# A decoder layer on one core: the feed-forward's low products behind a switch of TensorE, and the third norm's last step on GpSimd

## The chip, the core and the metric

The kernel runs on one core of one Trainium2 chip. A core has five engines with instruction streams of their own: TensorE (PE in the profile; its weight loads are PEld), VectorE (DVE), ScalarE (ACT), GpSimd (POOL) and SyncE (SP), which only issues transfers here. They wait for one another by semaphores. Sixteen DMA engines move data between the chip's memory and the on-chip memory, and they also bring the engines' instructions: the profile lists that traffic as queues of the kind "instruction". The metric is the device time of one execution in microseconds, and the time of a kernel is the median of its runs.

## The reference, cut to what matters

The layer computes, for 4 batches of 1024 tokens with 512 features in float32, an attention with 32 heads, a gated convolution, and a feed-forward, each added to its input and followed by a layer norm without learned scale. The part around the change is the feed-forward and the third norm:

```python
scale = jnp.maximum(act_scale, 1e-05)
x_int = jnp.clip(jnp.round(x / scale), -QB, QB)          # QB = 127
x_dq = jnp.nan_to_num(x_int * scale, nan=0.0, posinf=10000.0, neginf=-10000.0)
w = ternary_weight.astype(jnp.float32) - 1.0
return jnp.einsum('bsi,oi->bso', x_dq, w) + bias
...
x = _layernorm(x + _L0_ffn_ref(x, ternary_weight, bias, act_scale), axis=-1)
```

`ternary_weight` is an int32 array; the inputs drawn for it are 0, 1 or 2, so `w` is -1, 0 or 1.

## The kernel before, in words

`attention` takes the first 1700 us. `tail` does the rest, and it is written as one program of steps whose order is set by hand: `tail` enters a manual schedule, so each engine runs its instructions in the order in which the Python code issues them. A counter `now` is raised by `step()`, and `after(n, work)` puts work off by n steps; work that is due is issued at the end of the step, behind what the step itself issued.

`tail` goes twice over two batches, (0, 2) and then (1, 3). Each pass first runs the gated convolution: 32 gates for the two batches, one a step. `gate` (L1195 to L1216) gives TensorE four groups of 16 products into two pairs of PSUM buffers (`pc` and `pa`, two of each), then VectorE four additions (L1209, L1212, L1213, L1215), then ScalarE a sigmoid or tanh (L1216). After four gates `combine` spreads GpSimd, VectorE and ScalarE work over the next steps. Between, GpSimd makes sums of the next convolution weights (`sum_taps`, L196).

In the first pass, `halves_of_w_f` is issued along with the gates, one part at each of steps 17, 19, 21 and 23 and its last at step 25. For a quarter f of the feed-forward's weights, GpSimd copies the weights into the rounded type float32r (`w_hi`, L255) and subtracts that from the weights (L256), so that the remainder stands in `w_f`; SP writes it out (L257) and reads it back as `w_lo` (L261), also float32r.

Then comes `feed_forward` for the pass's two batches: 16 tiles of 128 tokens. For tile k the order of issue is:

- `turn` of tile k+1: four transposes on TensorE of the quantised tile `xq` (L1288) and ScalarE's copy of them from PSUM as float32r (`xq_t`, L1290);
- `feed` of tile k: eight products into one PSUM buffer `pf` (two buffers, tag "o"), four with `w_hi` and four with `w_lo` (L1298);
- `quantise` of tile k+3: ScalarE rounds (L1281), and VectorE (the first three) or GpSimd clamps (L1282);
- roots and aggregates of a finished group (`third_norm`'s `first`: L1314, L138);
- `residual` of tile k: VectorE adds the input (L1303) and takes the moments (L1304).

`third_norm` normalises in groups of four tiles (smaller at the end of a pass). Its `finish(m)` writes the normalised tile in place and has SP send it out (L1337). For even m ScalarE computes it as an activation with the scale `rstd` and the bias `shift` (L1332); for odd m VectorE computes it (`normalised`, L142). The very last tile is fed, added and finished in two halves of 256 columns.

After the first feed-forward, TensorE goes on with `project_out` (L292), whose PSUM buffers are the same two of tag "o".

Of the kernel before, what the change touches and what calls it, by code (L numbers as in the profile page):

```python
# [8 lines left out]
F32 = mybir.dt.float32  # L9
F32R = mybir.dt.float32r  # L10
AF = mybir.ActivationFunctionType
ALU = mybir.AluOpType
# [50 lines left out]
class Handed:  # L63
# [76 lines left out]

    def normalised(self, dst, src, mv, rstd, t):
        self.nc.vector.tensor_scalar(  # L142
            dst, src, mv[:, t, 0:1], rstd[:, t : t + 1], ALU.subtract, ALU.mult
        )
# [101 lines left out]

    def halves_of_w_f(self, pool, dram):


        nc, w = self.nc, self.w_f  # L250
        self.w_hi = pool.tile([P, FT, D], F32R, tag="w_hi", name="w_hi")
        low_d = dram.tile([P, FT, D], F32, tag="w_low", name="w_low_d")

        def part(f):
            nc.gpsimd.tensor_copy(self.w_hi[:, f, :], w[:, f, :])  # L255
            nc.gpsimd.tensor_sub(w[:, f, :], w[:, f, :], self.w_hi[:, f, :].bitcast(F32))  # L256
            nc.sync.dma_start(low_d[:, f, :], w[:, f, :])  # L257

        def last():
            self.w_lo = self.shared.tile([P, FT, D], F32R, tag="w_f", name="w_lo")  # L260
            nc.sync.dma_start(self.w_lo.bitcast(F32), low_d)  # L261

        return [lambda f=f: part(f) for f in range(FT)] + [last]

# [874 lines left out]
def tail(ctx, tc, a, out, ident, eps, hand, dram):  # L1139
# [153 lines left out]
    def feed(b, t, cols=slice(0, D)):  # L1293
        pt = ps_o.tile([P, D], F32, tag="o", name=f"pf{b}_{t}_{cols.start}")[:, 0 : cols.stop - cols.start]
        for n, w in enumerate((hand.w_hi, hand.w_lo)):
            for f in range(FT):
                last = n == 1 and f == FT - 1
                nc.tensor.matmul(pt, xq_ts[b, t][:, f, :], w[:, f, cols], start=n == f == 0, stop=last)  # L1298
        return pt
# [6 lines left out]
    def third_norm(b, n0, n):  # L1306
# [19 lines left out]
        def finish(m):  # L1326
            t = order[m]
            n = 2 if (b, m) == (B - 1, NT - 1) else 1
            for h in range(n):
                part = y[:, t, h * D // n : (h + 1) * D // n]  # L1330
                if m % 2 == 0 or h == 1:
                    nc.scalar.activation(  # L1332
                        part, part, AF.Identity, bias=made[2][:, m : m + 1], scale=made[0][:, m : m + 1]
                    )
                else:
                    hand.normalised(part, part, mv3[b], made[0], m)
# [73 lines left out]
    for m, work in enumerate(scaling):  # L1410
        after(9 + m, work)
    for m, work in enumerate(hand.halves_of_w_f(bigs, dram)):
        after(17 + 2 * m, work)
# [81 lines left out]
```

## Time and profile before

| what | value |
|---|---|
| median of 3 runs | 2144.36 us (2143.28, 2144.36, 2148.23) |
| the profiled execution | 2147.72 us, span of the profile 2145.8 us |
| granted TensorE clock, mean | 0.998 |
| first feed-forward, first to last product | 1854.97 to 1895.0 us |
| second feed-forward, first to last product | 2099.99 to 2140.12 us |
| products with `w_hi` and with `w_lo` | 132 and 132 |

The page's first part gives each engine's busy time. The second cuts the span into 40 slices. The third lists the DMA queues with packets, megabytes and their share of the sixteen engines' span. The fourth follows the chain of work that ended last. The groups, in the fifth, collect instructions by line, engine and tile, with the mean time of one, and then the idle time of the engine ahead of them with what ended it. The timeline lists instructions in order of time; the bracket at a line's end is idle time ahead of it and what ended it. Windows give each engine's busy time in a stretch. Matmul ends are modelled, so that consecutive matmuls overlap in the listing: their start-to-start distance is what counts.

### The profile page before, as it was taken

To read this page: it belongs to the slowest core of one execution; us is meant where nothing else is said; L and a number is where in the kernel's file an instruction comes from. 1 tells how busy PE (TensorE), PEld (TensorE's weight loads), DVE (VectorE), ACT (ScalarE), POOL (GpSimd) and SP (SyncE) were. 2 spreads that over 40 slices of the span, in tenths; PEclk is the share of its full clock that TensorE was granted. 3 is DMA by queue.
4 is the path that set the end of the run, shared out by engine and by line. 5 is a ranking of instruction groups with operands and counts; after the bars stand their busy time and mean duration, and the time that the engine had idled before them with its cause. 6 is when DMAs were issued, how large, how long until landed. Compare 5 with 4: busy or idle time off the path is not lost.

```text
span 2145.8 us, 81983 instructions
## 1 busy us (share of the span) xinstructions
PE 2109.5 (98%) x35404; PEld 1528.9 (71%) x35404; DVE 1728.0 (81%) x3068; ACT 1388.3 (65%) x2771; POOL 977.5 (46%) x1298
## 2 busy tenths in 40 slices
PE   9999999999999999999999999999999999999998
PEld 6666666666666666666666666667766799858997
DVE  3678888888888888888888888888897566779667
ACT  1157777777777777777777777777777623521336
POOL 2562534333344334343533333645464369532773
PEclk9999999999999999999999999999999999999999
DMA  7513213332322233122313124422411243270222
GB/s 274 176 52 98 78 50 92 106 123 64 102 54 78 63 103 107 60 88 88 106 54 111 54 75 132 147 64 84 123 47 52 60 163 118 74 279 21 100 78 79
DMA packets 114538, 207.97 MB, mean 97 GB/s; under 512 B 36992, under 2 KB 37248, under 8 KB 114048
## 3 DMA queue, kind: packets, MB, share of 16 engines
q1 hardware_dynamic: 113456, 201.55, 29.4%
q8 instruction: 277, 4.54, 0.9%
q10 hardware_dynamic: 720, 1.18, 0.2%
q14 instruction: 85, 0.70, 0.1%
HBM read 132.41 MB, written 69.73 MB: 94 GB/s over the span
## 4 chain that ended last, share of the span: by engine, by line
PE 84%; DVE 13%; POOL 1%; issue 1%; ACT 1%; DMA 0%; SPq 0%; DVEq 0%; ACTq 0%; POOLq 0%
PE av L872 23%; PE nat L758 15%; PE st L835 10%; DVE mx L771 9%; PE part L60 9%; PE pa L1205 6%; PE pc L1205 6%; PE v L60 5%; PE po L60 3%; PE po L292 3%; PE fold L425 1%; PE proj L60 1%; PE pf L1298 1%; PE fold L60 1%; DVE stats L1304 1%
## 5 line engine op out<-in xcount | busy, mean ns | idle before, releaser
L771 DVE TENSOR_REDUCE mx<-nat 128x1 f32<-128x512 f32 x2048 | 1271.4, 684 | 197.8 <-PE nat L758 179.5
L844 ACT ACTIVATE at<-st 128x512 f32<-128x512 f32 x2016 | 1042.2, 603 | 320.5 <-PE st L835 316.6
L758 PE MATMUL nat<-qk 32*128 32x512 f32 x4096 | 712.1, 421 | 2.2 <-DVE v_sb L658 1.3
L835 PE MATMUL st<-qk 32*128 32x256 f32 x8064 | 681.7, 290 | 0.2
L835 PEld LDWEIGHTS st<-qk 32*128 32x128 f32 x8064 | 526.1, 184 | 4.9 <-issue 2.1
L835 PE MATMUL st<-qk,ones 2*128 2x256 f32 x4032 | 504.1, 287 | 0.0
L872 PE MATMUL av<-at,v_sb 128*32 128x256 f32 x8192 | 499.4, 382 | 4.2 <-ACT at L844 1.3
L758 PEld LDWEIGHTS nat<-qk 32*128 32x128 f32 x4096 | 328.6, 184 | 203.0 <-DVE mx L771 162.6
L872 PEld LDWEIGHTS av<-at,v_sb 128*32 128x32 f32 x8192 | 240.8, 109 | 182.3 <-DVE mx L771 25.2
L835 PEld LDWEIGHTS st<-qk,ones 2*128 2x128 f32 x4032 | 353.6, 183 | 0.0
L1216 ACT ACTIVATE u<-u,b_c 128x512 f32<-128x512 f32 x64 | 46.2, 723 | 159.6 <-DVE u L1215 155.7
L778 POOL CAST neg<-least 128x16 fp32r<-128x16 f32 x64 | 12.7, 199 | 216.0 <-DVE least L776 216.0
L885 DVE TENSOR_TENSOR o_sb<-av,o_sb 128x256 f32<-128x256 f32 x128 | 54.4, 425 | 61.6 <-PE av L872 61.2
L722 POOL TENSOR_TENSOR y<-y,extra 128x256 f32<-128x256 f32 (+8 forms) x152 | 73.5, 518 | 65.9 <-ACT extra L708 65.9
L1212 DVE SCALAR_TENSOR_TENSOR u<-pa,u 128x342 f32<-128x342 f32 x64 | 40.6, 634 | 67.5 <-PE pa L1205 66.3
L921 POOL TENSOR_TENSOR o_n<-o_sb,o_n 128x512 f32<-128x512 f32 x64 | 83.3, 1324 | 13.3 <-DVE u L1213 13.3
L450 POOL TENSOR_TENSOR extra<-extra,highs 128x512 f32<-128x512 f32 x62 | 79.6, 1284 | 5.0
L1205 PE MATMUL pa<-xf,w 128*128 128x171 f32 x512 | 80.4, 308 | 0.5 <-POOL w L196 0.5
L1205 PE MATMUL pc<-xf,w 128*128 128x171 f32 x512 | 79.8, 308 | 0.0
L883 ACT COPY o_sb<-av 128x256 f32<-128x256 f32 x128 | 48.1, 376 | 46.9 <-PE av L872 36.7
L1205 PEld LDWEIGHTS pa<-xf,w 128*128 128x128 f32 x512 | 76.0, 189 | 1.0 <-POOL w L196 1.0
L1205 PEld LDWEIGHTS pc<-xf,w 128*128 128x128 f32 x512 | 76.0, 189 | 0.0
(210 smaller groups left out, 2782.3 us busy)
## 6 DMA issues: line engine op xcount, KB each, us to landing
qk<-qk_d SPq DMA_DIRECT2D x96, 512.0 KB
qk_d<-highs SPq DMA_DIRECT2D x96, 256.0 KB
qk_d<-extra SPq DMA_DIRECT2D x96, 256.0 KB
u<-in_ctx SPq DMA_DIRECT2D x16, 1024.0 KB
xT<-in_xT SPq DMA_DIRECT2D x16, 512.0 KB
o_n<-rec_d SPq DMA_DIRECT2D x128, 64.0 KB
attn<-o_n SPq DMA_DIRECT2D x256, 32.0 KB
y<-in_x SPq DMA_DIRECT2D x16, 512.0 KB
```

Of the source, the lines that this page charges most:

```text
L60: nc.tensor.matmul(pt[r, :], lhsT(f)[:, r], rhs(f), start=f == 0, stop=f == tiles - 1)
L292: nc.tensor.matmul(pt, attn_t[:, f, t * P : (t + 1) * P], self.w_o[:, f, :], start=f == 0, stop=f == FT - 1)
L450: eng.tensor_sub(block, block, high)
L722: eng.tensor_add(c, c, x)
L758: lambda n=n, r=r, turn=turn: nc.tensor.matmul(pts[n], qk_sets[u % 3][turn][r : r + 32, qt * P : (qt + 1) * P], qk_sets[u % 3][2][r : r + ...
L771: nc.vector.tensor_reduce(mxs[u][:, qt, j, kh : kh + 1], pts[n], AX.X, ALU.max, negate=True)
L835: lambda st=st, k=k, n=n, left=left, right=right: nc.tensor.matmul(st[:, k * QW : k * QW + QW], left, right, start=n == 0, stop=n == 2),
L844: nc.scalar.activation(at, st, AF.Exp, scale=0.25)
L872: nc.tensor.matmul(av[32 * j : 32 * j + 32, :], v_sb[b % 2][:, kt, c * VW : c * VW + 32], ats[u, 2 * i + n // 2, j][:, n % 2 * QW : n % 2 ...
L885: nc.vector.tensor_add(o, av, o)
L921: nc.gpsimd.tensor_mul(part, o_sb[:, cols].rearrange("p (s e) -> p e s", e=2), part)
L1205: nc.tensor.matmul(pt, w[i][:, tap, o : o + P], xf[:, tap, i, :], start=i == 0, stop=i == FT - 1)
```

## The change

The change has three parts.

First, `halves_of_w_f` has VectorE take, for each quarter f of the remainders, the largest value and the negated smallest (two reductions of 128x512). A new step `compare`, at step 27, reduces these eight columns to one, multiplies that column on TensorE with the column `magic` of equal positive numbers, which sums it over the partitions into one number, and has VectorE compare it with nought into an int32 flag. A new step `read`, at step 29, loads the flag into a register of TensorE's instruction stream.

Second, `feed` issues a hint of a switch, then three products with `w_hi`, then a switch on the register with two arms. Arm 0 holds the fourth product with `w_hi` and nothing else. Arm 1 holds that product and the four with `w_lo`. Which arm runs is known only when the kernel runs; with the weights given, whole numbers from -1 to 1, the remainders are nought if the rounded type holds these numbers exactly. There are 33 calls of `feed`: 15 whole tiles and two halves in the second pass, 16 in the first.

Third, `finish` gives the last step of the third norm to GpSimd, as a subtraction and a multiplication with per-partition operands, for all tiles of batches 0, 1 and 2 and the first four of batch 3: 28 tiles, of which ScalarE and VectorE had 14 each. The last four tiles of batch 3 stay as they were.

```diff
-    def normalised(self, dst, src, mv, rstd, t):
-        self.nc.vector.tensor_scalar(
+    def normalised(self, dst, src, mv, rstd, t, eng=None):
+        (eng or self.nc.vector).tensor_scalar(
             dst, src, mv[:, t, 0:1], rstd[:, t : t + 1], ALU.subtract, ALU.mult
         )
...
-    def halves_of_w_f(self, pool, dram):
+    def halves_of_w_f(self, pool, dram, ps):
         nc, w = self.nc, self.w_f
+        lows = self.shared.tile([P, 2 * FT + 1], F32, tag="lows", name="lows")
+        flag = self.shared.tile([1, 1], mybir.dt.int32, tag="flag", name="flag")
...
             nc.gpsimd.tensor_copy(self.w_hi[:, f, :], w[:, f, :])
             nc.gpsimd.tensor_sub(w[:, f, :], w[:, f, :], self.w_hi[:, f, :].bitcast(F32))
             nc.sync.dma_start(low_d[:, f, :], w[:, f, :])
+            nc.vector.tensor_reduce(lows[:, f : f + 1], w[:, f, :], AX.X, ALU.max)
+            nc.vector.tensor_reduce(lows[:, FT + f : FT + f + 1], w[:, f, :], AX.X, ALU.min, negate=True)
+
+        def compare():
+            top = lows[:, 2 * FT : 2 * FT + 1]
+            nc.vector.tensor_reduce(top, lows[:, 0 : 2 * FT], AX.X, ALU.max)
+            pt = ps.tile([P, FT, P], F32, tag="t", name="any_low")[0:1, 0, 0:1]
+            nc.tensor.matmul(pt, top, self.magic, start=True, stop=True)
+            nc.vector.tensor_scalar(flag, pt, 0.0, None, ALU.is_gt)
+
+        def read():
+            engine = mybir.EngineType.PE
+            why = "a comparison gives nought or one"
+            self.any_low = {
+                engine: nc.values_load(
+                    flag, engines=[engine], min_val=0, max_val=1, skip_runtime_bounds_check_because=why
+                )
+            }
...
-        return [lambda f=f: part(f) for f in range(FT)] + [last]
+        return [lambda f=f: part(f) for f in range(FT)] + [last, compare, read]
...
         pt = ps_o.tile([P, D], F32, tag="o", name=f"pf{b}_{t}_{cols.start}")[:, 0 : cols.stop - cols.start]
-        for n, w in enumerate((hand.w_hi, hand.w_lo)):
-            for f in range(FT):
-                last = n == 1 and f == FT - 1
-                nc.tensor.matmul(pt, xq_ts[b, t][:, f, :], w[:, f, cols], start=n == f == 0, stop=last)
+        tc.switch_hint(hand.any_low, 2, label=f"low{b}_{t}_{cols.start}")
+        def product(w, f, start=False, stop=False):
+            nc.tensor.matmul(pt, xq_ts[b, t][:, f, :], w[:, f, cols], start=start, stop=stop)
+
+        for f in range(FT - 1):
+            product(hand.w_hi, f, start=f == 0)
+        for arm in tc.Switch(hand.any_low, n=2, hint=f"low{b}_{t}_{cols.start}"):
+            product(hand.w_hi, FT - 1, stop=arm == 0)
+            if arm:
+                for f in range(FT):
+                    product(hand.w_lo, f, stop=f == FT - 1)
         return pt
...
-                if m % 2 == 0 or h == 1:
+                if b != B - 1 or m < 4:
+                    hand.normalised(part, part, mv3[b], made[0], m, nc.gpsimd)
+                elif m % 2 == 0 or h == 1:
...
-    for m, work in enumerate(hand.halves_of_w_f(bigs, dram)):
+    for m, work in enumerate(hand.halves_of_w_f(bigs, dram, ps_t)):
         after(17 + 2 * m, work)
```

## The prediction

> **What bounds the kernel now.** I read the page first: busy times, DMA queues, the chain that ended last.
>
> ```profile
> PE 2109.5 (98%) x35404; PEld 1528.9 (71%) x35404; DVE 1728.0 (81%) x3068; ACT 1388.3 (65%) x2771; POOL 977.5 (46%) x1298
> q8 instruction: 277, 4.54, 0.9%
> PE 84%; DVE 13%; POOL 1%; issue 1%; ACT 1%; DMA 0%; SPq 0%; DVEq 0%; ACTq 0%; POOLq 0%
> ```
>
> TensorE (PE) carries the chain. Queue q8 is TensorE's code: 35404 products and as many weight loads over 277 packets are 256 instructions a packet, so a packet is one block of code (16 KB). 0.9% of sixteen engines over 2145.8 us is 309 us, or 1.1 us a packet. It is fetched while the code runs straight on, and nearly nothing waits for it (issue 1%).
>
> Next the two feed-forwards as windows (columns: TensorE, weight loads, DVE, ACT, POOL, clock, DMA share, GB/s), then the groups in the first and TensorE's timeline of one tile.
>
> ```profile
> 1854.97:1895.00 40.03, 37.31 (x187) 29.58 (x187) 35.36 (x79) 29.76 (x46) 18.16 (x20) 1.00 0.43 149
> 2099.99:2140.12 40.13, 37.42 (x194) 29.82 (x193) 35.66 (x79) 29.86 (x46) 18.09 (x19) 1.00 0.19 71
> ```
>
> ```profile
> L1303 DVE SCALAR_TENSOR_TENSOR y<-pf,sc,big 128x512 f32<-128x512 f32 x15 | 11.1, 739 | 1.5 <-PE pf L1298 1.5
> L1304 DVE BATCH_NORM_STATS2 stats<-y 128x6 f32<-128x512 f32 x15 | 10.4, 695 | 0.5
> L1282 POOL TENSOR_SCALAR xq<-xq 128x512 f32<-128x512 f32 x10 | 6.4, 641 | 8.5 <-ACT xq L1281 8.1
> L142 DVE TENSOR_SCALAR y<-y,mv,rstd 128x512 f32<-128x512 f32 x11 | 6.0, 561 | 0.1
> L1332 ACT ACTIVATE y<-y,shift,rstd 128x512 f32<-128x512 f32 x7 | 5.6, 806 | 0.7 <-DVE shift L1321 0.7
> ```
>
> ```profile
> 1870.82 0.60 PE L1288 MATMUL tr<-ident,xq 128*128 128x128 f32 x4
> 1871.18 1.16 PE L1298 MATMUL pf<-w_hi,xq_t 128*128 128x512 f32 x4
> 1872.18 1.09 PE L1298 MATMUL pf<-w_lo,xq_t 128*128 128x512 f32 x4
> 1873.11 0.60 PE L1288 MATMUL tr<-ident,xq 128*128 128x128 f32 x4
> ```
>
> A tile takes 2.29 us, start to start: transposes 0.36, high products 1.00, low ones 0.93. VectorE is close behind, 35.36 of 40.03 us busy.
>
> **The change, part by part.** *Removed:* the remainders of -1, 0 and 1 are nought if the rounding keeps whole numbers, as I assume; arm 0 runs. TensorE loses 128 products of 512 columns and 4 of 256: 31 tiles by 0.93 and two halves by 0.46, 29.8 us. That is a bound, not the gain: without them a tile needs 1.36 us of TensorE, while VectorE needs 0.74 + 0.69 and its share of aggregates, about 1.7.
>
> *Third norm's last step:* 28 tiles go to POOL, 14 from ACT (0.81 each), 14 from VectorE (0.53): 8 of each in the first feed-forward, 6 in the second. POOL's price lies between its clamp, 0.64, and its two-input addition in the same window, 1.34; I take 0.64, the same operation with two scalars. The first feed-forward gives POOL 18.16 + 16 x 0.64 = 28.4 us of 40 (39.6 by the high price); the clamp of a later tile queues behind it, and POOL now waits 8.1 us there for ACT. SP's output transfer waits for POOL instead. Hidden, gain on the path nought unless TensorE has become faster than VectorE.
>
> *The flag.* Eight reductions of 128x512 on VectorE (L771's 0.68 each, 5.5 us) in a stage where TensorE is the bound. Their place costs more: each pair stands in VectorE's order behind a gate's additions and waits for POOL's subtraction.
>
> ```profile
> 1803.01 0.88 DVE L1215 SCALAR_TENSOR_TENSOR u<-pa,u 128x513 f32<-128x513 f32 x1
> 1804.39 0.64 DVE L1209 TENSOR_TENSOR u<-pc,u 128x342 f32<-128x342 f32 x1 [0.49 <-PE pc L1205]
> 1807.38 1.28 POOL L256 TENSOR_TENSOR w_f<-w_f,w_hi 128x512 f32<-128x512 f32 x1
> 1819.73 1.98 PE L1205 MATMUL pa<-xf,w 128*128 128x171 f32 x10 [0.49 <-POOL w L196]
> ```
>
> The third pair would be due about 1804 and can't start before 1808.7; the gates' next additions queue behind it, ACT's gate functions behind those, POOL's `combine` behind these and its weight sums (L196) last, for which TensorE already waits 0.49 us. TensorE is two gates (9.3 us) ahead at most by its buffers. From 0 (all absorbed) to 8 us (two delays of 4 in full); I take 4, the middle, as the last row has no slack and the buffers have some. `compare`: TensorE's small product follows gate 27 at once but needs VectorE's 0.64 + 0.40 + 0.88 and a small reduction (0.19) first: 2.1 us of standing, 2.3 with handing over. `read`: no row; between 0 and the 1.9 us of the last output's round trip below; I take 1. Sum: 7.3 us, 2 to 12.
>
> *The switch.* Before has no branch, so neither a jump's price nor where the arms lie can be seen. I assume that an arm and the code behind the switch lie outside the straight line, each in another block: 33 ways in and 33 out, none visited twice. Lower bound of a jump: 0.05 us, what TensorE's sequencer takes for one step (51 ns in the row below). Upper bound: a block's whole fetch. A transfer that someone waits for is at the end:
>
> ```profile
> 2143.23 0.36 ACTq L1337 DMA_DIRECT2D out<-y  x1
> L1491 SPq DRAIN  x3: 7/7/13, 2145.1 to 2145.4; - x3
> L1491 PEldq EVENT_SEMAPHORE  x2: 51/51/51, 2145.3 to 2145.8; - x2
> ```
>
> SP passes its wait for this last output at 2145.1: 1.9 us from issue to landing, for 128 KB spread over sixteen engines. A block goes through one engine in 1.1 us; with 1.2 us of the 1.9 for starting and signalling I estimate a fetch at 2.3 us. If a packet ahead of it in the queue has to pass first (the block next in line, say), 3.4.
>
> The hint stands only three products ahead of the way in, under 1 us of issuing, and the way out can be known only inside the arm, which holds one product (0.23 us). So I let both fetches stand in the sequencer's path, one after the other: 2 x 2.3 + 0.1 for the jumps = 4.7 us a switch, against 2.29 for the whole tile now. The tile's own 1.36 us of TensorE work, VectorE's 1.7 and POOL's 1.3 run meanwhile and cost nothing; if fetches were free, VectorE would be late next.
>
> First feed-forward: 16 x 4.7 = 75.2, less 2.3 for a gate's group already queued on TensorE when its sequencer meets the first switch, 72.9 against 40.0: +32.9. Second: 17 x 4.7 - 2.3 = 77.6 against 40.1: +37.5. With the flag +77.7, against the profiled execution's 2147.7 (span 2145.8 and 1.9 around it). The median of the runs is 3.3 lower; from it, 2144.4 + 77 = **2221 us**.
>
> [...]
>
> **The rivals.**
>
> *Each fetch has to let another packet pass.* Both jumps at 3.4: 66 x 1.1 = +73, so 2294. For it: two fetches may be called for at once, the next in line and the hinted one; against it: sixteen engines could take them side by side.
>
> *Only the way out waits*, the arm being the next block in line. 2.3 us at least, 3.7 with the tile's own work behind it; at 3.0: 16 x 3 - 2.3 - 40.0 = +5.7, 17 x 3 - 2.3 - 40.1 = +8.6, with the flag +21.6: 2166. For it: code ahead is fetched without being asked.
>
> *The jumps don't show; VectorE becomes the bound* (the other side). First feed-forward: 35.36 - 8 x 0.53 = 31.1 busy, with its present 1.5 us of waits for `pf` 32.6: -7.4. Second: 35.66 - 6 x 0.53 + 1.5 = 34.0: -6.1. With the flag -6.2: 2138; 2133 to 2143 by the flag's bounds. For it: a hint exists to bring code early. It decides if a switch takes less than about 2.3 us of the sequencer, i.e. a jump under 1.1 us, one packet's own duration.
>
> That the switch leaves the low products running (remainders not nought) would be as the forecast with 29.8 us of TensorE work more, mostly inside the waits; I give it no chance of its own.
>
> **How the numbers follow.** Forecast 0.45, slower fetches 0.15, one fetch 0.17, no fetch 0.23. The forecast's own range is 2185 to 2260: a fetch of 1.8 to 2.8 is 33 us either way, the flag's bounds are inside. For 8 in 10 the low end lies in the last rival, near its middle, 2136 (a tenth below), the high end at 2300, past the slow fetch's centre (under a tenth above). A measurement tells 0.2%, 4.3 us, from no change. Faster is two thirds of the last rival, 0.16; same the rest of it, 0.07; slower 0.77.
>
> **What would show it.** TensorE's code queue: some 66 to 100 packets more than 277. In the feed-forwards, TensorE's idle time per tile of about 3.3 us with nothing named ahead of it but issue, in two places: ahead of the fourth high product and ahead of the next transposes; windows of about 73 and 78 us; VectorE waiting for `pf`. No product with `w_lo`. In the gates, VectorE waiting for `w_f`, TensorE for `w` and for `lows`, a few us. Right about the work but wrong about the price: tiles at 1.7 to 2.0 us with VectorE nearly always busy. The prediction fails if the arms are already there when TensorE jumps, or if a fetch costs far from 2.3 us.

## The result, and the profile after

The changed kernel takes 2344.5 us, the median of four runs (2342.12 to 2347.96), against 2144.94 for the kernel before on the same chip: 1.093 times as long, 95% interval 1.091 to 1.0949. The forecast was 2221 with 2136 to 2300 as its range. So it is slower, as foretold, but by 200 us and not by 77. The profiled execution took 2344.2 us, with a span of 2342.4.

First the page: engines, granted clock, TensorE's code queue, the chain that ended last.

```profile
PE 2130.8 (91%) x35274; PEld 1525.2 (65%) x35274; DVE 1724.2 (74%) x3064; ACT 1379.3 (59%) x2757; POOL 1033.7 (44%) x1326
...
PEclk9999999999999999999999999999999855999855
...
q8 instruction: 374, 6.13, 1.2%
...
PE 77%; DVE 12%; issue 6%; POOL 4%; ACT 1%; POOLq 0%; DMA 0%; SPq 0%; DVEq 0%; ACTq 0%
```

TensorE has 130 instructions less than before, 35274 for 35404: the 132 products with `w_lo` don't run, and the flag's small product is there in two records. Its code queue carried 97 packets more than 277. In the chain, "issue" has gone from 1% to 6%: time in which TensorE waits for nothing that the profile names. GpSimd has gone from 1% to 4%.

Then the two feed-forwards as windows (columns as in the prediction: TensorE, weight loads, DVE, ACT, POOL, clock, DMA share, GB/s).

```profile
1857.95:1993.00 135.05, 47.61 (x122) 27.23 (x121) 33.50 (x78) 25.85 (x40) 49.17 (x36) 0.52 0.23 74
2205.00:2340.00 135.00, 46.93 (x120) 27.38 (x120) 32.49 (x77) 26.91 (x42) 42.14 (x31) 0.51 0.12 36
```

135 us each, where they were 40. No engine is busy for more than 49 of them, so none is the bound. The granted clock is 0.52 and 0.51 where it was 1.00, and a product takes 0.68 us and not 0.41; but that too is inside time in which TensorE mostly stands.

The groups of the first feed-forward:

```profile
L1319 PE MATMUL pf<-w_hi,xq_t 128*128 128x512 f32 x64 | 37.1, 681 | 28.2 <-issue 28.2
L142 POOL TENSOR_SCALAR y<-y,mv,rstd 128x512 f32<-128x512 f32 x16 | 33.1, 2074 | 16.8 <-DVE rstd L139 16.3
...
L1310 PE MATMUL tr<-ident,xq 128*128 128x128 f32 x56 | 15.1, 423 | 56.4 <-issue 52.1 <-POOL y L142 4.3
L1332 DVE SCALAR_TENSOR_TENSOR y<-pf,sc,big 128x512 f32<-128x512 f32 x16 | 12.0, 750 | 92.8 <-PE pf L1319 86.7 <-POOL y L142 6.1
...
L1304 POOL TENSOR_SCALAR xq<-xq 128x512 f32<-128x512 f32 x10 | 6.1, 613 | 61.5 <-ACT xq L1303 61.5
```

The last number of a line is idle time ahead of these instructions, and what ended it. TensorE is idle 28.2 us ahead of high products and 56.4 us ahead of transposes, nearly all put down to issue. VectorE is idle 92.8 us, mostly for `pf`. And GpSimd's new step takes 2.07 us a tile, where the forecast had 0.64 and an upper bound of 1.34.

TensorE's timeline, three tiles (start, duration; in the brackets idle time ahead and its releaser):

```profile
1877.72 1.12 PE L1310 MATMUL tr<-ident,xq 128*128 128x128 f32 x4 [4.16 <-issue]
1878.49 1.63 PE L1319 MATMUL pf<-w_hi,xq_t 128*128 128x512 f32 x3
1881.04 0.79 PE L1319 MATMUL pf<-w_hi,xq_t 128*128 128x512 f32 x1 [0.92 <-issue]
1885.77 1.11 PE L1310 MATMUL tr<-ident,xq 128*128 128x128 f32 x4 [3.94 <-issue]
1886.53 1.63 PE L1319 MATMUL pf<-w_hi,xq_t 128*128 128x512 f32 x3
1889.24 0.79 PE L1319 MATMUL pf<-w_hi,xq_t 128*128 128x512 f32 x1 [1.08 <-issue]
1894.11 1.12 PE L1310 MATMUL tr<-ident,xq 128*128 128x128 f32 x4 [4.08 <-issue]
```

A tile takes 8.05 and 8.34 us, start to start. The two gaps stand where the forecast put them, ahead of the fourth high product and ahead of the next transposes, and the second is four times the first. What lies in them shows in the branches of TensorE's sequencer (PEldq; min/median/max in ns):

```profile
L1522 PEldq COMPARE_BRANCH  x66: 317/4575/5928, 1856.3 to 2336.1; - x66
```

Taken in turn, the 33 ways in have a median of 2.25 us and the 33 ways out 4.85.

For the accounts, and for the experiments below, one table of stages from the profiled execution of each kernel, in us: the gates of the first pass up to the first product of the feed-forward; the feed-forward up to the first product of `project_out`; that, up to the next gate; the gates of the second pass; its feed-forward up to its last product; the end.

| kernel | gates | feed-forward 1 | project_out | gates | feed-forward 2 | end | median time |
|---|---|---|---|---|---|---|---|
| before | 155.1 | 40.0 | 54.9 | 150.1 | 39.9 | 6.0 | 2144.94 |
| the change | 160.4 | 136.3 | 57.5 | 150.1 | 134.3 | 6.3 | 2344.5 |
| arms swapped | 161.6 | 137.6 | 57.2 | 150.1 | 136.1 | 8.2 | 2352.19 |
| one arm | 161.1 | 43.7 | 65.4 | 150.1 | 43.9 | 11.4 | 2177.98 |
| no hint | 161.5 | 133.5 | 57.7 | 150.1 | 130.1 | 6.3 | 2339.74 |
| straight, new norm | 153.0 | 44.4 | 64.3 | 150.1 | 43.8 | 11.7 | 2169.38 |
| straight, old norm | 153.2 | 37.6 | 56.4 | 150.1 | 37.2 | 6.9 | 2141.47 |
| new norm alone | 153.3 | 45.1 | 62.8 | 150.1 | 45.1 | 10.0 | 2166.67 |
| flag alone | 164.0 | 40.0 | 54.9 | 150.1 | 39.9 | 6.0 | 2152.82 |
| switch, old norm | 161.7 | 138.0 | 57.1 | 150.1 | 135.5 | 5.9 | 2345.71 |
| all in the arm | 160.0 | 135.8 | 58.0 | 150.1 | 128.8 | 5.9 | 2340.13 |
| pairs | 161.9 | 80.0 | 57.1 | 150.1 | 79.1 | 5.9 | 2234.72 |
| mixed norm | 153.2 | 38.6 | 55.5 | 150.1 | 37.2 | 6.9 | 2142.88 |
| skip | 161.5 | 44.8 | 64.5 | 150.1 | 44.5 | 11.6 | 2178.56 |

The attention ahead of these stages ends between 1697.0 and 1702.7 us in all of them, with the same code and without order among them; in the change's profile it is 2.4 us shorter than in the profile before. Beside that, the change's 196.6 us more of span are 96.3 and 94.4 in the feed-forwards, 5.3 in the first gates, 2.6 in `project_out` and 0.3 at the end. So the question for the experiments is what the two jumps of a switch are made of.

### The profile page after: what moved, and what is told of

Read it like the earlier page. It is cut to its first block, busy times and chain, and to the rows that moved or that the text cites. A ratio compares the mean times of both kernels' runs of the same rounds, so it can differ in the third digit from the quotient of the medians.

```text
span 2342.4 us, 82260 instructions
## 1 busy us (share of the span) xinstructions
PE 2130.8 (91%) x35274; PEld 1525.2 (65%) x35274; DVE 1724.2 (74%) x3064; ACT 1379.3 (59%) x2757; POOL 1033.7 (44%) x1326
## 4 chain that ended last, share of the span: by engine, by line
PE 77%; DVE 12%; issue 6%; POOL 4%; ACT 1%; POOLq 0%; DMA 0%; SPq 0%; DVEq 0%; ACTq 0%
PE av L894 21%; PE nat L780 14%; PE st L857 9%; PE part L60 9%; DVE mx L793 8%; PE pc L1227 5%; PE pa L1227 5%; PE v L60 4%; PE po L314 2%; PE po L60 2%; POOL y L142 2%; PE tr L1310 1%; PE fold L447 1%; PE proj L60 1%; PE pf L1319 1%
## 5 line engine op out<-in xcount | busy, mean ns | idle before, releaser
L1332 DVE SCALAR_TENSOR_TENSOR y<-pf,sc,big 128x512 f32<-128x512 f32 (+1 forms) x33 | 24.2, 734 | 187.4 <-PE pf L1319 181.3
L1310 PE MATMUL tr<-ident,xq 128*128 128x128 f32 x128 | 32.3, 404 | 112.1 <-issue 103.9
L1319 PE MATMUL pf<-w_hi,xq_t 128*128 128x512 f32 (+1 forms) x132 | 74.6, 665 | 59.2 <-issue 59.2
L1312 ACT ACTIVATE xq_t<-tr,unmagic 128x512 fp32r<-128x512 f32 x32 | 21.7, 685 | 170.3 <-PE tr L1310 170.3
L1310 PEld LDWEIGHTS tr<-ident,xq 128*128 128x128 f32 x128 | 21.3, 202 | 126.0 <-issue 116.8
L1319 PEld LDWEIGHTS pf<-w_hi,xq_t 128*128 128x128 f32 x132 | 36.1, 304 | 84.9 <-issue 82.1
```

Source lines behind the costliest of these rows:

```text
L1310: nc.tensor.transpose(tr[:, f, :], xqs[b, t][:, f * P : (f + 1) * P], ident)
```

## The experiments

Twelve kernels ran. Ratios are against the kernel before on the same chip, with 95% intervals.

### Which jump is dear: the arms swapped

```diff
-            nc.vector.tensor_scalar(flag, pt, 0.0, None, ALU.is_gt)
+            nc.vector.tensor_scalar(flag, pt, 0.0, None, ALU.is_le)
...
-            product(hand.w_hi, FT - 1, stop=arm == 0)
-            if arm:
+            product(hand.w_hi, FT - 1, stop=arm == 1)
+            if arm == 0:
```

> The two arms change places: the flag is turned round (1 where all remainders are nought), arm 0 holds the low products and arm 1 the fourth high product alone, so the arm that runs is the second and the code behind the switch is the block next in line to it. Theory of the neighbour's packet (a jump waits about 2.25 us for its block when that is the next in line and comes alone, and about 4.85 us when the next in line is fetched beside it): way in 4.3 to 4.9 us, way out 2.2 to 2.8 us, time 2344 within 20 us. Theory of the late hint (the way out is dear because its hint stands right ahead of the jump): way out still about 4.85 us, way in between 2.25 and 4.85 us, time 2344 to 2430 us.

Measured: 2352.19 us, ratio 1.0965 (1.0933 to 1.0997). The way in has a median of 3.97 us now, the way out 3.06; together 7.03, where the change has 7.1. The dear jump has changed sides, as the first theory says. Its numbers (4.3 to 4.9 and 2.2 to 2.8) were both missed, since the time that a jump stands leaves out what the sequencer does ahead of it; the table below counts from the entry into a block. The hint for the way out stands where it stood, so its lateness is not what made that jump dear.

What did shows in the trace's records of the code queue. The table takes, for each jump, the moment when TensorE's sequencer enters a block (the end of the jump before) and says how many packets start before the next jump is done, when the jump is reached, how long it stands, when the next block is entered, and how long after the jump is reached the second packet starts; medians over the switches of a kernel without the first of each pass, in us. It has the kernels of three later experiments too.

```
kernel          jump     packets   entry to jump   jump stands   entry to entry   second after jump
the change      way in      1          1.08            2.26           3.34               -
the change      way out     2          0.18            4.86           5.04               0.98
arms swapped    way in      2          1.08            3.99           5.09               0.98
arms swapped    way out     1          0.17            3.06           3.23               -
no hint         way in      1          0.48            2.71           3.28               -
no hint         way out     2          0.18            4.79           4.96               0.98
all in the arm  way in      1          0.95            2.29           3.24               -
all in the arm  way out     2          0.28            4.60           4.86               1.00
pairs           way in      1          2.28            1.11           3.23               -
pairs           way out     2          0.18            4.75           4.98               1.01
```

A jump with one packet takes 3.2 to 3.3 us from entry to entry, one with two 4.9 to 5.1, in each of the five kernels. The first packet starts 0.73 to 0.76 us after entry in all of them. Alone it takes about 1.0 us; where there are two, the change's take 1.5 and 1.9. From the last packet's landing, 1.4 us (one packet) or 1.4 to 1.8 (two) pass until the sequencer goes on. In the order of the kernel's code the arm that runs in the change comes next after the block with the hint, and its jump has one packet; the end lies one arm further, and then a second packet comes beside the first. With the arms swapped it is the other way round.

The last column tells what calls for the second packet. It starts 1.0 us after the jump is reached (0.9 at the least, in each of these kernels), whether the jump stands 0.18 or 1.08 us behind the entry, and whether the last hint stands 0.12 us ahead of the jump (the change, way out) or 0.50 (arms swapped, way in). So the first packet comes with the entry and the second with the jump, and neither with a hint. With the swapped arms it starts later after entry than in the change, 2.07 us against 1.16, and yet the next block is entered as soon: it then takes 1.5 us and not 1.9, and the sequencer goes on 1.4 us after its landing and not 1.8. That the first packet is the block next in line and the second the target is inferred from this and from the exchange of the arms; the records of packets don't say which block they carry.

### A switch with one arm

```diff
-                    flag, engines=[engine], min_val=0, max_val=1, skip_runtime_bounds_check_because=why
+                    flag, engines=[engine], min_val=0, max_val=0, skip_runtime_bounds_check_because=why
...
-        tc.switch_hint(hand.any_low, 2, label=f"low{b}_{t}_{cols.start}")
+        tc.switch_hint(hand.any_low, 1, label=f"low{b}_{t}_{cols.start}")
...
-        for arm in tc.Switch(hand.any_low, n=2, hint=f"low{b}_{t}_{cols.start}"):
+        for arm in tc.Switch(hand.any_low, n=1, hint=f"low{b}_{t}_{cols.start}"):
```

> The switch has one arm, the fourth high product; the low products are left out altogether. The code behind the switch is then the next block in line to the arm. Theory of the neighbour's packet: way in 2.25 us as now, way out 2.2 to 2.8 us in place of 4.85 us, 33 times 2.1 to 2.6 us less: 2258 to 2275 us. Theory of the late hint: way out as now, 2344 us.

Measured: 2177.98 us, ratio 1.0153 (1.0124 to 1.0183), 276 code packets and no compare-and-branch in the trace. The switch of one arm left no jump behind here, so neither theory's time (2258 to 2275, 2344) was put to the test, and this run says nothing on two fetches at once. It says something else: what the rest of the change costs. With the flag, GpSimd's norm and no low products, but no jumps, the kernel takes 33.1 us more than before; the jumps take the other 166.5, which is 5.0 us for each of 33 switches on top of what a tile takes without them.

### The hint

```diff
-        tc.switch_hint(hand.any_low, 2, label=f"low{b}_{t}_{cols.start}")
...
-        for arm in tc.Switch(hand.any_low, n=2, hint=f"low{b}_{t}_{cols.start}"):
+        for arm in tc.Switch(hand.any_low, n=2):
```

> The hint ahead of the first product is left out; the arms keep their own hint of the way out. If the next block in line is fetched at a block's entry anyway, the way in is as now or a little dearer at the jump, since the jump comes about 0.5 us sooner: 2330 to 2350 us. If the hint is what starts the fetch, it starts about 0.5 us later, at the jump: 2355 to 2375 us. If without it the block is fetched late and with more to do, as 4.85 us a way in: 2420 to 2440 us.

Measured: 2339.74 us, ratio 1.0907 (1.0876 to 1.0939). The packet for the way in starts as early after entry without a hint as with one (0.73 and 0.75 us), so nothing of this fetch, of an arm that is next in line, was due to the hint. (The arms' own hint of the way out stayed in; by the table's last column it starts nothing either.) Without it the jump is reached 0.6 us sooner and stands 0.45 us longer. The hint gains nothing here; the kernel without it is 4.8 us quicker by the medians, with intervals that overlap.

### What the rest costs: straight code, part by part

Four kernels without any switch. The first leaves out flag, switch and low products and has the new norm; the second the same with the norm as before; the third is the kernel before with the new norm alone; the fourth the kernel before with the flag alone, computed and read and used for nothing.

```diff
-        for n, w in enumerate((hand.w_hi, hand.w_lo)):
-            for f in range(FT):
-                last = n == 1 and f == FT - 1
-                nc.tensor.matmul(pt, xq_ts[b, t][:, f, :], w[:, f, cols], start=n == f == 0, stop=last)
+        for f in range(FT):
+            nc.tensor.matmul(pt, xq_ts[b, t][:, f, :], hand.w_hi[:, f, cols], start=f == 0, stop=f == FT - 1)
```

> No flag, no switch: four high products a tile in straight code, the low products left out; the third norm's last step on GpSimd as in the change. It is the change with a switch that costs nothing. Theory of GpSimd as the bound (its step took 2.07 us in the changed kernel, so 18.2 + 16 x 2.07 = 51 us in the first feed-forward and 18.1 + 12 x 2.07 = 43 us in the second, against 40 before): 2150 to 2158 us, though part of it may lag into the next stage. Theory of VectorE as the bound, as the prediction's last rival had it: 2131 us.

> The same straight code without the low products, the third norm's last step on ScalarE and VectorE as before. VectorE's 35.4 us and its waits of 1.5 us bound the first feed-forward, 35.7 and 1.5 the second: 3 us less in each, 2139 us. If TensorE still sets the pace by its chain with ScalarE and the clamp, 2130 us or less is out of reach and 2145 us is the other end.

```diff
-                if m % 2 == 0 or h == 1:
+                if b != B - 1 or m < 4:
+                    hand.normalised(part, part, mv3[b], made[0], m, nc.gpsimd)
+                elif m % 2 == 0 or h == 1:
```

> The third norm's last step on GpSimd alone, low products as before. Theory of GpSimd as the bound with 2.07 us a tile: the clamp queues behind it, TensorE waits for it, 2150 to 2160 us. By the prediction's price of 0.64 us: hidden, 2145 us.

```diff
+            nc.vector.tensor_reduce(lows[:, f : f + 1], w[:, f, :], AX.X, ALU.max)
+            nc.vector.tensor_reduce(lows[:, FT + f : FT + f + 1], w[:, f, :], AX.X, ALU.min, negate=True)
...
+        return [lambda f=f: part(f) for f in range(FT)] + [last, compare, read]
```

> The flag alone: the reductions, the comparison and the register load, with the feed-forward and the norm as before. By the changed kernel's profile, where the first product of the feed-forward started 2.98 us later than before: 2148 us. By the prediction's term of 7.3 us: 2152 us.

Measured:

| kernel | median us | ratio | less the kernel before |
|---|---|---|---|
| straight, new norm | 2169.38 | 1.0121 (1.0107 to 1.0135) | +24.7 |
| straight, old norm | 2141.47 | 0.9983 (0.9974 to 0.9992) | -3.2 |
| new norm alone | 2166.67 | 1.0106 (1.0092 to 1.012) | +22.0 |
| flag alone | 2152.82 | 1.0041 (1.0027 to 1.0055) | +8.1 |

What had been put down beforehand holds for the flag alone (2152, not 2148) and nearly for the straight kernel with the old norm (2139). It fails for both kernels with the new norm, which take longer than either theory had it: GpSimd is late, as one of the theories says, but its lag goes on past the feed-forward.

So leaving out the low products is worth 3.2 us of the 29.8 that TensorE spends on them. In the straight kernel with the old norm, the first feed-forward takes 37.6 us, 34.6 of which VectorE is busy, and TensorE 26.9:

```profile
1851.20:1888.80 37.60, 26.88 (x123) 18.13 (x123) 34.59 (x77) 28.69 (x45) 18.07 (x20) 0.95 0.42 151
```

The new norm costs 22.0 us, and not only in the feed-forwards: by the table of stages 5.1 and 5.2 there, 7.9 in `project_out` and 4.0 at the end. The kernel with the new norm alone shows the way it goes. GpSimd's timeline, from the middle of the first feed-forward, which ends at 1895.7:

```profile
1884.59 2.07 POOL L142 TENSOR_SCALAR y<-y,mv,rstd 128x512 f32<-128x512 f32 x1
1886.74 0.61 POOL L1282 TENSOR_SCALAR xq<-xq 128x512 f32<-128x512 f32 x1
1887.43 1.28 POOL L1260 TENSOR_TENSOR big<-y,b_f 128x512 f32<-128x512 f32 x1
1888.71 2.08 POOL L142 TENSOR_SCALAR y<-y,mv,rstd 128x512 f32<-128x512 f32 x1
1890.86 0.61 POOL L1282 TENSOR_SCALAR xq<-xq 128x512 f32<-128x512 f32 x1
1891.58 18.52 POOL L142 TENSOR_SCALAR y<-y,mv,rstd 128x512 f32<-128x512 f32 x9
```

GpSimd works without a gap; the clamps (L1282) stand in its order behind steps of 2.07 us, and when the last clamp is done nine normalisations are left, 18.5 us, of which 14.4 reach past the end of the feed-forward. Who waits for it, in the kernel with the new norm alone: TensorE in the feed-forward, SP's queue from 1890 to 1920 us, with the order of its transfers from 1895 on, and then VectorE and TensorE in `project_out`.

```profile
PE tr L1288 <- POOL xq L1282: 5.3, 7, 1.6
```

```profile
SPq L1339 <- POOL y L142: 17.1, 9, 3.7
```

```profile
1895.74 6.50 SPq L1339 DMA_DIRECT2D out<-y  x4
1902.40 1.95 SPq L117 DMA_DIRECT2D y<-in_x  x4
1904.45 6.01 SPq L1339 DMA_DIRECT2D out<-y  x4
```

```profile
DVE y L296 <- DMA y<-in_x: 7.7, 1, 7.7
...
PE po L292 <- DVE y L297: 5.4, 1, 5.4
```

and in the kernel before, from 1895 to 1950 us:

```profile
DVE y L296 <- DMA y<-in_x: 0.9, 1, 0.9
```

TensorE's transposes wait for the clamp. SP's output transfers wait 17.1 us for GpSimd, and the loads of the input for `project_out` stand behind them in SP's order; VectorE waits 7.7 us for such a load, and TensorE 5.4 us for VectorE. In the kernel before, VectorE waits 0.9 us for such a load, no product in `project_out` waits for another engine, and no transpose waits for a clamp by GpSimd. At the end of the kernel SP's last output transfers wait 18.0 us for GpSimd in the same way; its last steps run to 2159.8 us, 6.0 behind the last product's start, and the kernel ends at 2163.8.

The flag costs 8.1 us, and by the table of stages only the first gates are longer. The waits there, the same in the kernel with the flag alone and in the change; these are the change's, from 1775 to 1858 us:

```profile
DVE lows L262 <- POOL w_f L260: 10.4, 2, 5.9
...
PE any_low L269 <- DVE lows L267: 4.1, 1, 4.1
...
PE pc L1227 <- DVE u L1231: 1.1, 1, 1.1
...
PE pa L1227 <- POOL w L196: 0.8, 1, 0.8
```

VectorE's reductions wait 10.4 us for GpSimd's subtractions, and TensorE in turn 4.1 us for the last reduction. Reading the flag takes the sequencer 0.49 us:

```profile
L276 PEldq TENSOR_LOAD <-flag x1: 487/487/487, 1840.6 to 1840.6; - x1
```

### Do the norm and the switch add up?

The change with the first lines of `finish` as before (the diff of the new norm, undone).

> The flag and the switch as in the change, but the third norm's last step shared by ScalarE and VectorE as before. The norm's step on GpSimd alone cost 22 us (2166.7 against 2144.7). Theory: beside switches it is hidden, since GpSimd's 2.07 us a tile is far less than a tile's 8.2, so putting it back gains nothing: 2340 to 2346. Rival: the two costs add, 2344.5 less 22 is 2322. A gain in between would say that GpSimd's late tiles still hold up the work behind the first feed-forward or the end of the kernel.

Measured: 2345.71 us, ratio 1.0939 (1.0919 to 1.0959). The 22 us of the norm are not to be had beside the switches: where a tile takes eight, GpSimd's 2.07 are free, and `project_out` and the end take what they take in the change. Put differently, without the jumps the norm would have been the change's largest cost.

### From when a fetch runs

Three high products more in the arm, then one switch for two tiles.

```diff
-        for f in range(FT - 1):
-            product(hand.w_hi, f, start=f == 0)
         for arm in tc.Switch(hand.any_low, n=2, hint=f"low{b}_{t}_{cols.start}"):
-            product(hand.w_hi, FT - 1, stop=arm == 0)
+            for f in range(FT):
+                product(hand.w_hi, f, start=f == 0, stop=arm == 0 and f == FT - 1)
```

> The change, with the first three high products of a tile moved from ahead of the switch into both arms, so that the arm that runs has all four. It tells from when a fetch runs. Theory: the next blocks are called for when TensorE's sequencer enters a block, so that what stands in a block ahead of its jump runs beside the fetch; the way in then waits longer by the issue of three products (about 0.7 us: from 2.25 to 2.9) and the way out less by as much (from 4.85 to 4.1 or 4.2), the tile stays at 8.2 us and the time at 2340 to 2350. Rival: the way out's packets are called for by its jump, so work ahead of it hides nothing; the way out stays at 4.85, the way in still grows, a tile takes 8.9 us, the kernel 33 x 0.7 = 23 us more, 2367.

Measured: 2340.13 us, ratio 1.0913 (1.0893 to 1.0933). The time is the theory's and not the rival's, but the test was weak: three products take TensorE's sequencer only some 0.1 us (in the table of jumps, entry to jump goes from 1.08 to 0.95 and from 0.18 to 0.28), not the 0.7 that I had put down, though TensorE is busy with three for 1.63 us (the change's timeline). The way out stands 0.26 us less, the way in as before. So the time of this run leaves open from when the way out's fetch runs; the starts of the packets tell it, and neither side had it whole: the first packet comes with the entry, as the theory has it, and the second with the jump (1.00 us after it is reached), as the rival has it.

```diff
-    def feed(b, t, cols=slice(0, D)):
+    def feed(b, t, cols=slice(0, D), more=False):
...
+        open_tiles.append((b, t, pt))
...
+        if more:
+            return pt
+        for arm in tc.Switch(hand.any_low, n=2, hint=labels[-1]):
+            for tile in open_tiles:
+                product(tile, hand.w_hi, FT - 1, stop=arm == 0)
...
-                pt = feed(b, t)
+                more = k % 2 == 0 and k < len(tiles) - 2
+                pt = feed(b, t, more=more)
...
-                residual(b, n, t, pt)
+                waiting.append((b, n, t, pt))
+                if not more:
+                    for one in waiting:
+                        residual(*one)
+                    waiting = []
```

> The change with one switch for two tiles: the first three high products of both tiles stand ahead of it, the last product of each in the arms; the additions of both tiles follow on VectorE. The last two tiles of a pass keep switches of their own: 19 switches, not 33. Theory that a tile's work runs beside the fetch: a pair takes the 8.2 us of a tile, or up to 9.5 where the second tile's copy out of PSUM (two buffers) stands in the way; 14 switches less give 14 x 8.2 = 115 to 14 x 6.9 = 97 us less: 2230 to 2248. Rival, that a switch adds its 5.0 us (166.5 us over 33, change against the one-arm kernel) to whatever the tiles take: 14 x 5.0 = 70 less, 2274. VectorE's 1.43 us of addition and moments a tile is 2.9 a pair, no bound in either case.

Measured: 2234.72 us, ratio 1.0422 (1.0402 to 1.0441): 109.8 us less than the change for 14 switches less, 7.8 each, inside the theory's range and far from the rival's 2274. TensorE's timeline of a pair:

```profile
1901.64 1.11 PE L1310 MATMUL tr<-ident,xq 128*128 128x128 f32 x4 [5.52 <-issue]
1902.40 1.63 PE L1324 MATMUL pf<-w_hi,xq_t 128*128 128x512 f32 x3
1903.83 1.05 PE L1310 MATMUL tr<-ident,xq 128*128 128x128 f32 x4
1904.54 2.09 PE L1324 MATMUL pf<-w_hi,xq_t 128*128 128x512 f32 x5
1909.67 1.12 PE L1310 MATMUL tr<-ident,xq 128*128 128x128 f32 x4 [3.04 <-POOL xq L1304]
```

Two tiles, eight transposes and eight products, in 8.03 us: what one took. (Over the nine switches of the first pass it is 8.9 each, 80.0 us; GpSimd's steps are among the releasers of the longer ones.) The table of jumps says why: the way in is reached 2.28 us after entry instead of 1.08, and stands 1.11 instead of 2.26. The way in's packet starts 0.73 to 0.76 us after the entry, and 1.2 us more of work ahead of its jump cost nothing: 3.23 us from entry to entry, where the change has 3.34. That up to some 3.2 us of work would be free there is an estimate from these numbers. For a jump past a block no kernel here has more than 1.08 us ahead of it; its second packet starts 1.0 us after the jump is reached.

### Is it the jump or its target?

```diff
-        tc.switch_hint(hand.any_low, 2, label=f"low{b}_{t}_{cols.start}")
...
-        for f in range(FT - 1):
-            product(hand.w_hi, f, start=f == 0)
-        for arm in tc.Switch(hand.any_low, n=2, hint=f"low{b}_{t}_{cols.start}"):
-            product(hand.w_hi, FT - 1, stop=arm == 0)
-            if arm:
-                for f in range(FT):
-                    product(hand.w_lo, f, stop=f == FT - 1)
+        for f in range(FT):
+            product(hand.w_hi, f, start=f == 0, stop=f == FT - 1)
+        with tc.If(hand.any_low[mybir.EngineType.PE] > 0):
+            for f in range(FT):
+                product(hand.w_lo, f, stop=f == FT - 1)
```

> The change with a conditional block in place of the two-armed switch: all four high products stand ahead of it, and the four low products inside are jumped over when the flag is nought. So there is one taken jump a tile, over a few instructions, and no arms in blocks of their own. It tells whether the price belongs to a taken jump as such or to a target in another block. Theory: a target that is already there costs no fetch; the time is that of the change with a free switch (one-arm kernel, 2178), give or take 5: 2173 to 2183, and TensorE's code packets stay near 277. Rival one: any taken jump calls for a fetch of one packet, 3.3 us from the entry into a block as for the way in; a tile's 2.7 us of straight work hide in it, so 33 x 0.6 = 20 us more: 2198. Rival two: the block next in line is fetched beside it as on the way out, 5.0 a tile: 33 x 2.3 = 76 more, 2254.

Measured: 2178.56 us, ratio 1.0156 (1.0133 to 1.0179): the 2178 of the change with a free switch. The page's code queue and the branches of TensorE's sequencer:

```profile
q8 instruction: 278, 4.55, 0.9%
```

```profile
L1322 PEldq COMPARE_BRANCH  x33: 202/207/353, 1858.9 to 2164.3; - x33
```

33 jumps over the four low products take 0.21 us each, and one code packet more than before is fetched, not 97. The same decision, on the same flag, with the same work done: the 166 us go with the two arms and their 97 packets, not with a jump as such. Since this kernel still has the flag and the new norm, it stays 33 us above the kernel before.

### Towards a quicker kernel

The straight kernel with the old norm is the only one that beats the kernel before, by 0.17%. It gives up what the flag was for: with weights that the rounded type doesn't hold exactly, the low products would be missing. One more kernel tried to take load off its VectorE.

```diff
-                if m % 2 == 0 or h == 1:
+                if m in (1, 5) and b != B - 1:
+                    hand.normalised(part, part, mv3[b], made[0], m, nc.gpsimd)
+                elif m % 2 == 0 or h == 1:
```

> No flag, no switch, the low products left out (for weights of -1, 0 and 1 they are nought), and of the third norm's last step four tiles a pass go from VectorE to GpSimd, in the first pass and in the first half of the second (six in all); the rest stays as before. The same without this move took 2141.5, with VectorE as the bound of a feed-forward of 37.6 us. Theory: VectorE has 4 x 0.56 = 2.2 us less in the first feed-forward and 1.1 in the second, GpSimd 8.3 us more of its slack: 2138 to 2140. Rival: GpSimd's clamp of a later tile waits behind the 2.07 us step as it did with all sixteen tiles, and the time is 2142 to 2148.

Measured: 2142.88 us, ratio 0.9994 (0.9985 to 1.0003). In its profile the first feed-forward is longer by 1.0 us, not shorter by 2.2: the rival's side, at its lower end. So four steps of 2.07 us on GpSimd gained nothing; whether they cost something is not clear, since by the medians it is 1.4 us and the intervals of the two kernels overlap.

## Why the prediction was right or wrong

**Right: the direction and where the time goes.** TensorE's sequencer fetches code twice a tile, one fetch after the other; the packets (97 more, 66 to 100 foretold, which is nearly three a switch where the sum had two), the two places of idle time, their releaser "issue", VectorE's wait for `pf` and the absence of products with `w_lo` are as foretold. The tile's own work is hidden in the waits, as it was costed.

**Wrong: the price of a switch, 4.7 us, made of 2 x 2.3 for fetches and 0.1 for the jumps.** It is 8.4, by the medians 3.34 for the way in and 5.04 for the way out. The way in's fetch stands 2.26 us, which looks like the 2.3 of the forecast; but the whole from entry to entry is 3.3, and the 2.26 is only what is left of it after 1.08 us of other steps, which the forecast had at nothing. The way out stands 4.86 us, some 2.5 more than its term, and has a second packet that the forecast didn't have. The forecast had taken 1.1 us for a packet and 1.2 for starting and signalling from the last output's transfer. The trace shows for one packet 0.75 to its start, 1.0 in the queue and 1.4 from landing to going on, 3.2 in all; the transfer was the nearest row, but a row of another queue, and it was 0.9 us short. Over 33 switches, 8.4 in place of 4.7 would be 122 us. By stages, 72.9 was foretold and 136.3 measured, and 77.6 and 134.3: 120.1 of the miss of 123.5. (The sum added 77.7 as 77, too little to matter.)

**The first rival had the mechanism that the forecast left out,** a packet beside the one that is wanted, and counted 3.4 for both jumps. It is so for the way out alone, and that jump costs 5.0: the second packet starts 1.2 us after entry and not 0.75, it takes 1.9 us beside the first and not 1.0, and the sequencer goes on 1.8 us after the last landing and not 1.4. The rival had the two called for at once, by the hint; the second starts 1.0 us after the jump is reached. A sum by its mechanism with the right sizes would have been above the range's high end, which had been set by 3.4.

**The upper bound was no bound.** "A block's whole fetch" was taken as the highest price of a jump, 3.4 with a packet ahead. The wait runs from entry (3.34 and 5.04 us) and includes the time after landing (1.4 to 1.8 us), for which no row of before stood. That unknown should have kept the high end open; a round trip of 1.9 us gave a false certainty.

**The hint was right to be given nothing.** The forecast let it come too late; the run without it shows that it wasn't late but without effect: the next block is called for 0.73 us after entry anyway. For a jump past a block, hints up to 0.5 us ahead of it had none either; an earlier one wasn't tried.

**The third norm was costed at nothing, hidden, with 0.64 a step.** The step takes 2.07 us, above its upper bound of 1.34. The row that was taken, the clamp, works with two constants and clamps; the step subtracts and multiplies with two operands per partition from tiles, and the trace before had no such step on GpSimd. Which of the two differences makes it slow, no run separates. Hidden it was, but only because the switch made tiles long enough: alone it costs 22.0 us. The forecast did name the wait of SP's output transfers for GpSimd, and didn't ask what stands behind them in SP's order: loads for `project_out`. That is the queue that it should have followed.

**The flag was sized well, in part by luck.** 7.3 us with 2 to 12 was foretold, and 8.1 measured alone; in the change's profile its gates are 5.3 us longer than before. Inside the sum, the compare's wait is larger (4.1 us for the reduction where 2.1 of standing was put down) and the read smaller (0.49 where 1 was). The hold-up by the eight reductions, put at 4 us, shows on TensorE as 1.1 us of waiting for VectorE and 0.8 for the weight sums, where 0.5 stood before. What else makes up the 8.1 isn't shown.

**The rival on the other side was half right about what lies behind the jumps.** It had VectorE as the bound without them, -13.5 us for the feed-forwards with the norm's VectorE share gone to GpSimd. With the norm where it was, straight code is 3.2 us quicker, VectorE busy for 34.6 of the first feed-forward's 37.6 us; with the norm on GpSimd it is 24.7 slower, since GpSimd, not VectorE, is late next: from 1850 to 1900 us TensorE's transposes wait 11.6 us for GpSimd's clamp and 4.0 for VectorE's. So that rival's time, 2138, could not have come even if the jumps were free: the kernel with the skip shows 2178.6.

**Two runs tell the prices of a jump apart.** In the change, where the arms make 97 code packets more, a jump costs 3.3 or 5.0 us from entry to entry; in the skip, over four products and with one packet more, it takes 0.21.

## What to carry to other kernels

A switch with two arms was paid for in code fetches, here 3.3 us for an arm next in line and 5.0 us to get past another arm, not in jumps; where one side is empty, a conditional block that is jumped over cost 0.21, here with four products in it. If there must be two arms, put work into the block ahead of the way in (2.28 us of it were free here, of 3.2 from entry to entry), and make one switch serve several tiles (14 switches less gave 7.8 us each); the way past an arm had its second packet only 1.0 us after its jump was reached. And before work is moved to an engine with time to spare, find a row of that very operation, operands included, and read on from the engine to the queues that wait for it: here output transfers waited 17.1 us for GpSimd, and VectorE 7.7 us for a load that stood behind them in SP's order.

## What the runs showed of the hardware

- In the five kernels with two arms, a packet of TensorE's code starts 0.73 to 0.76 us (medians) after the sequencer enters a block, with and without a hint. Where the jump passes over an arm, a second one starts 1.0 us after the jump is reached, with the last hint 0.12 to 0.50 us ahead of the jump.
- Between the landing of a code packet that comes alone (1.0 us in the queue) and the sequencer's going on lie another 1.4 us; where there are two, 1.4 to 1.8.
- The kernel whose switch has one arm shows no compare-and-branch in its trace, and 276 code packets.
- GpSimd's subtraction and multiplication with two per-partition operands takes 2.07 us on 128x512, and VectorE's same step 0.56; GpSimd's clamp with two constants takes 0.61 to 0.64, and VectorE's 0.62 in the change's first feed-forward and 0.95 in that of the kernel before.
- The granted clock was 0.52 and 0.51 in the feed-forwards of the change, where TensorE was busy for 47.6 and 46.9 of 135 us; 0.95 in the first one of the straight kernel with the old norm, with 26.9 of 37.6; and 1.00 before, with 37.3 of 40.0. A product took 0.68 us in the change and 0.41 before; the jumps, 3.3 and 5.0 us, were longer than the products that ran beside them.
